# A four-layer graph network whose PSUM banks are dealt out anew: four banks in turn for the work outside the recurrence, one bank shared inside it, and residual sums in pieces

## The chip, the cores and the metric

The kernel runs on one core of a Trainium2 chip. The metric is the device time of one execution in microseconds. The kernel before takes 1431.12 us, the median of three runs (1428.45 to 1432.41).

## What is computed

128 batches of 64 nodes with 256 features pass through four layers. Each layer normalises its input, clips it at zero, computes one graph operation on it and adds the result to its input (the residual sum). Everything is float32.

```python
for layer in (attention_4_heads, attention_1_head, relations, gated_recurrence):
    h = maximum(layernorm(x), 0)
    x = x + layer(h, adj, weights)          # the residual sum

# attention: Wh = h @ W; softmax over the neighbours; elu(attention @ Wh)
# relations: adj is 0 or 1 here, so that only relation 1 is ever met
# gated_recurrence, three steps on the same adjacency A:
    m    = h @ weight[i]
    aggr = A^T @ m
    r = sigmoid(aggr @ Wir + h @ Whr + b)
    z = sigmoid(aggr @ Wiz + h @ Whz + b)
    n = tanh(aggr @ Win + b + r * (h @ Whn + b))
    h = (1 - z) * n + z * h
```

## The kernel before

The rows of all graphs are laid on 128 partitions and taken in 16 groups of four tiles of 128 rows. Per group, the first three layers and the preparation of the recurrence are called "the work outside the recurrence" here. The recurrence of group g runs in three steps, each in two chunks `a` and `b` of 128 output features. Outside work of later groups is placed beside it.

The order in which each engine does its instructions is worked out when the program is built. A planner notes all operations with what they depend on, and then emits, again and again, the one that can start first by its own account of time; among equals the one that is due first. LATENCY, the start and end of each job and its `spread` set those dues. On the chip each engine runs its list in order and waits at semaphores.

PSUM has eight banks of 512 float32 per partition. Five belong to the recurrence, one to each kind of product; three (`mt`) are dealt out in turn to everything else. Until the recurrence is first used, the outside work may also have four of the five.

```python
class Banks(Pool):
    own = ("ry", "rm", "rz", "nh", "ni")
    early = psum = True

    def room(self, tag, base):
        return 3 if tag == "mt" else 1

    def tile(self, shape, dtype, name, **kwargs):
        view = super().tile(shape, dtype, name, **kwargs)
        view.base.whole = name not in self.own     # (*)
        return view

    def place(self, base, taken):
        if base.tag in self.own:
            return super().place(base, taken)
        for tag in ("mt", *self.own[: 4 if 115.0 else 5]) if self.early else ("mt",):
            ...
psum = Banks(..., 1, Banks.own)        # tags in `own` are taken in the order asked for
```

(*) The first TensorE operation on a bank that is marked `whole` waits until the inputs of all TensorE operations on it are there, so that the bank is held shortly. Banks of the recurrence aren't marked: their products are emitted one by one.

In a chunk, `r` (the reset gate) of the first half of the columns, S0, is made from two products in the bank `rm` and two in `ry`, one of each from h and one from the messages. Seven such pairs of products serve both gates of both halves; `ry` is added to over and over and copied out in between, `rz` takes two more. `nh` and `ni` are the two parts of n, from h and from the aggregated messages. Each call of `mul` is one 256-column product, which the chip does as two matmul instructions; each call of `gate` is one of 512 columns, also as two.

```python
class Chunk:
    def __init__(...):
        self.r, self.t, self.z, self.d = (work.tile([P, T], F32, name=name) for name in "rtzd")   # one buffer each

    def bank(self, name):
        if name in self.banks:
            return self.banks[name], False
        self.banks[name] = psum.tile([P, T], F32, name=name)
        return self.banks[name], True

    def nh_there(self):                                 # ScalarE reads nh into t
        nc.scalar.activation(self.t, self.banks["nh"], AF.Identity, bias=bh[...])

    def r_there(self, h):
        r, t = self.r[:, h], self.t[:, h]
        if h == S0:
            nc.vector.tensor_tensor(r, self.banks["rm"][:, S0], r, ALU.add)     # VectorE reads rm
            y = r
        else:
            y = self.banks["ry"][:, S0]
        nc.scalar.activation(r, y, AF.Tanh, bias=brz[...], scale=0.5)
        nc.vector.scalar_tensor_tensor(t, r, 1.0, t, op0=ALU.add, op1=ALU.mult)
    # n_there: t += ni, tanh, d = h - t (GpSimd);  z_there: rz, tanh
    # h_there: d = (z + 1) * d; hnew = d * 0.5 + t

# one step of the recurrence, in the order in which the banks are asked for (cut)
a.mul("ry", 1, 0); a.gate("nh", 0)
...; a.gate("ni", 0); ...; a.gate("nh", 1); a.nh_there()
a.mul("rm", 2, 0) + a.mul("rz", 7, 0); a.mul("rm", 2, 1)
a.r_there(S0); ...; a.both("ry", 6); a.m16_there()
b.both("rm", 2)                                         # b asks for rm first
a.both("ry", 5); ...; b.gate("nh", 0)                   # and for nh after it
a.both("ry", 3); a.r_there(S1); ...; a.h_there(S1); ...; a.h_there(S0)
b.gate("nh", 1); b.nh_there(); b.both("ry", 1); b.m1_there(); b.r_there(S0)
...
```

The two attention layers end with elu and the residual sum, 128x1024 elements for a whole group. From the second group on GpSimd does the sum:

```python
def elu_add(work, src, o, engine, by_scalar=False):
    ...
    nc.vector.scalar_tensor_tensor(em, em, -1.0, o, op0=ALU.add, op1=ALU.max)
    engine.tensor_tensor(src, src, em, ALU.add)
```

Of the kernel before, what the change touches and what calls it, by code (L numbers as in the profile page):

```python
# [8 lines left out]
F32 = mybir.dt.float32  # L9
I32 = mybir.dt.int32  # L10
AF = mybir.ActivationFunctionType
ALU = mybir.AluOpType
# [4 lines left out]
P = 128  # L17
# [3 lines left out]
G = 4  # L21
T = G * P
# [26 lines left out]
class View:  # L49


    def __init__(self, base, shape, steps=(), region=None, live=None):
        self.base, self.shape, self.steps, self.region, self.live = base, tuple(shape), steps, region, live
# [83 lines left out]
class Pool:  # L137
# [3 lines left out]
    psum = False  # L141
# [21 lines left out]
    def released(self, tag, base, before):  # L163
# [3 lines left out]
        if before < 0:  # L167
            return 0.0
        return sorted(b.end for b in live if not b.left)[before] + Plan.LATENCY

# [29 lines left out]
class Job:  # L200
# [2 lines left out]

    def __init__(self, start, end, after):
        self.start, self.end, self.after, self.left, self.length = start, end, after, 0, 0.0
        self.spread = 1.86


class Plan:

    LATENCY = 170.8

    def __init__(self, nc):
        self.nc, self.on, self.ops, self.job = nc, False, [], None
# [51 lines left out]
    def emit(self):  # L268
# [20 lines left out]
        for op in reversed(self.ops):  # L289
            if op.job.end is None:  # L290
                op.due = 1e9
                for t in op.then:
                    late = 0.0 if t.engine == op.engine else self.LATENCY
                    op.due = min(op.due, t.due - op.job.spread * (op.cost + late))
# [8 lines left out]
        def enter(op):  # L303
            t = 0.0
            for other, data in op.after.items():
                late = other.end + self.LATENCY
                if other.engine == op.engine and not (other.dma and data):
# [137 lines left out]
def kernel(  # L445
# [28 lines left out]
    nc = Plan(tc.nc)  # L474
# [141 lines left out]
    def elu_add(work, src, o, engine, by_scalar=False):  # L616

        em = work.tile(list(o.shape), F32, name="em")
        if by_scalar:
            nc.scalar.activation(em, o, AF.Relu, scale=-1.0)  # L620
            nc.scalar.activation(em, em, AF.Exp, scale=-1.0)
        else:
            nc.vector.tensor_scalar(em, o, 0.0, None, op0=ALU.min)
            nc.scalar.activation(em, em, AF.Exp)
        nc.vector.scalar_tensor_tensor(em, em, -1.0, o, op0=ALU.add, op1=ALU.max)
        engine.tensor_tensor(src, src, em, ALU.add)

    def block_diagonal(dst, src, scalar, op):

# [131 lines left out]
    def recurrence(work, psum, start, src, abd, store, in_parts=False):  # L761
# [16 lines left out]
        class Chunk:  # L778
# [8 lines left out]
            def bank(self, name):  # L787

                if name in self.banks:
                    return self.banks[name], False  # L790
                self.banks[name] = psum.tile([P, T], F32, name=name)
                return self.banks[name], True

            def mul(self, name, q, source):
# [157 lines left out]
    with ExitStack() as s1:  # L952
# [4 lines left out]
        class Banks(Pool):  # L957

            own = ("ry", "rm", "rz", "nh", "ni")
            early = psum = True

            def room(self, tag, base):
                return 3 if tag == "mt" else 1

            def tile(self, shape, dtype, name, **kwargs):
                view = super().tile(shape, dtype, name, **kwargs)
# [3 lines left out]
            def place(self, base, taken):  # L972
                if base.tag in self.own:
                    return super().place(base, taken)
                for tag in ("mt", *self.own[: 4 if 115.0 else 5]) if self.early else ("mt",):
                    live = sum(1 for b in self.live.get(tag, ()) if b.left)
                    if live + taken.count(tag) < self.room(tag, base):
                        return tag
                return None
# [7 lines left out]
        psum = Banks(s1.enter_context(tc.tile_pool(name="psum", bufs=1, space=PSUM)), 1, Banks.own)  # L987
# [29 lines left out]
        def load_group(g):  # L1017
            nc.begin(("load", g))
            xg = work.tile([P, G, D], F32, name="xg", bufs=6)
            n = 2 if g == 0 else G  # L1020
            for p in range(0, G, n):
                nc.sync.dma_start(xg[:, p : p + n], xr[:, g * G + p : g * G + p + n, :])
            at = work.tile([P, G // 2, 2, N], I32, name="at", bufs=3)
            for a in range(2):
                for u in range(G // 2):
                    edges = tr[g * G // 2 + u, a]
                    nc.sync.dma_start(at[a * N : (a + 1) * N, u], edges)
            AT.append(at)
            XG.append(xg)
# [71 lines left out]
        def attention(g, p0, n, layer, heads, we, pool):  # L1101
# [49 lines left out]
            for q in range(0, n, m):  # L1151
# [5 lines left out]
                nc.vector.tensor_tensor(t4, t4, edges, ALU.min)  # L1157
            o = aggregate_graphs(pool, psum, t, wv, heads, g < 16)
            elu_add(pool, src, o, nc.vector if g < 1 else nc.gpsimd, g < 0)

        def first_weights():
# [84 lines left out]
        def before(g):  # L1246
            ABD[g] = work.tile([P, G, N], F32, name="abd")
            START[g] = before_recurrence(W[3], psum, XG[g], AG[g], ABD[g], g >= AHEAD)

        def recur(g):  # L1250
            recurrence(
                W[3], psum, START.pop(g), XG[g], ABD[g],
                lambda h, part: nc.sync.dma_start(outr[:, g * G : (g + 1) * G, :][part], h[part]),
                g == NG - 1,
            )
# [3 lines left out]
        nc.begin("weights", 18.0, 0 or None)  # L1259
        later_weights(early)  # L1260
        layers = (first_layer, second_layer, third_layer)
        start, period = 87.96, 83.9
        users = {}
        for g in range(NG):
            if g > 1:
                load_group(g)

            if g == 0:
                units = [(0, 2, (-2.5, 24.3, 61.4, 71.1)), (2, 2, (-2.7, 25.3, 58.8, 74.4))]
            elif g == 1:  # L1270
                units = [(0, 2, (24.1, 54.4, 87.6, 97.3)), (2, 2, (45.5, 67.3, 98.2, 128.1))]
            elif g == 2:
                units = [(0, G, (74.5, 120.77, 176.8, 238.5))]
            else:
                end = start + g * period - 32.8
                units = [(0, G, [end - 53.2 * i + x for i, x in ((3, 0.0), (2, -0.95), (1, -4.68), (0, 0.0))])]
            for p0, n, at in units:
                spare = g == 0 and p0 > 0
                for i in range(3):
                    end = None if g < 2 else at[i + 1]  # L1280
                    nc.begin((g, p0, i), at[i], end, [users[i]] if i in users and not spare else [])
                    if g > 1:
                        nc.job.spread = 3.0
                    if not spare:
                        users[i] = (g, p0, i)
                    layers[i](g, p0, n, spare)
            if g == 0:
                nc.begin("make")
                nc.note("-", make_gru, 0.0, [], [], [op for op in nc.ops if any(b.pool is early for b in op.bases)])
            at = start + g * period  # L1290
            nc.begin(("before", g), at - (13.0 if g == 0 else 21.1), at, [("recur", g - 2)] if g > 1 else [])
            before(g)
            nc.begin(("recur", g), at, at + period)
            recur(g)
# [58 lines left out]
    def general_attention(X):  # L1353

        with ExitStack() as s3:
# [16 lines left out]
            for layer, heads, we in ((0, H, w0e), (1, 1, w1e)):  # L1372
                pool = Plain(str(layer))
                gh = G * heads
                with tc.For_i(0, NP, G) as p0:
# [40 lines left out]
                    for c in range(0, gh, 4):  # L1416
# [3 lines left out]
                        nc.vector.tensor_copy(ec[:, c : c + 4, :].rearrange("p h i -> p (h i)"), pt)  # L1420
                    o = aggregate(pool, psum, lambda p, h: ec[:, p * heads + h, :], wv, heads)
                    elu_add(pool, src, o, nc.gpsimd)
                    nc.sync.dma_start(X[:, bass.ds(p0, G), :], src)

# [115 lines left out]
```

## Time and profile before

| What | Value |
|---|---|
| Time, median of three | 1431.12 us |
| Span of the profiled execution | 1428.7 us |
| TensorE (PE) | busy 1403.0 us, 98% of the span, 9703 matmul instructions |
| VectorE (DVE) | busy 1027.9 us, 72% |
| ScalarE (ACT) | busy 808.1 us, 57% |
| GpSimd (POOL) | busy 600.5 us, 42% |
| TensorE clock granted | 0.997 |
| DMA | 67.89 MB, 48 GB/s |
| First product of the recurrence of the first and second group | 91.7 us, 191.1 us |
| and of the last group | 1349.7 us |

A busy share is the time in which at least one instruction of that engine is under way. The ends of matmuls are modelled and reach over the start of the next one, so that PE at 98% still has short gaps that the share hides: the distance between the starts of two matmuls tells more. In the lists of groups each line gives engine, operation, output<-inputs, shape and count, then busy time and the mean time of one in ns, then the idle time just before them and what ended it.

From some 190 us on the groups follow each other every 82 to 84.5 us; the last group has no outside work left to put beside its recurrence.

### The profile page before, as it was taken

The numbers are of one execution on the slowest core, as the hardware profiler recorded it, in microseconds if no ns is written. First come the engines' busy times: TensorE is split into PE (matmuls) and PEld (weight loads), VectorE is DVE, ScalarE is ACT, GpSimd is POOL, SyncE is SP. The second block draws the span as 40 slices with busy tenths as digits, with TensorE's granted clock in tenths as the row PEclk, the third lists the DMA queues.
The fourth block names the chain that finished last, engine by engine and source line by source line (L and its number), as shares of the span: only waits on it lengthen the run. The fifth ranks groups of instructions, "written<-read, shape, count | busy, mean of one in ns | idle before, by whom it ended". The sixth has DMA issues, their size and how long they took to land.

```text
span 1428.7 us, 27951 instructions
## 1 busy us (share of the span) xinstructions
PE 1403.0 (98%) x9703; PEld 964.6 (68%) x9703; DVE 1027.9 (72%) x2553; ACT 808.1 (57%) x2045; POOL 600.5 (42%) x744
## 2 busy tenths in 40 slices
PE   9999999999999999999999999999999999999997
PEld 8666666767667666766766676676667666666664
DVE  6658677785958869685886968688686958665544
ACT  3665556565555655655565565556556555554543
POOL 1454344445424444543444354344435434352422
PEclk9999999999999999999999999999999999999998
DMA  8010222222223122222312222231212122111000
GB/s 219 22 20 20 42 60 37 59 44 41 61 49 71 32 63 42 45 60 49 72 31 63 42 46 60 48 72 30 59 28 44 45 45 54 26 22 28 16 15 18
DMA packets 299420, 67.89 MB, mean 48 GB/s; under 512 B 274696, under 2 KB 297480, under 8 KB 299272
## 3 DMA queue, kind: packets, MB, share of 16 engines
q1 hardware_dynamic: 298712, 65.50, 22.0%
q8 instruction: 80, 1.31, 0.4%
q14 instruction: 68, 0.56, 0.1%
q10 hardware_dynamic: 560, 0.52, 0.1%
HBM read 28.06 MB, written 8.53 MB: 26 GB/s over the span
## 4 chain that ended last, share of the span: by engine, by line
PE 88%; DVE 5%; ACT 2%; DMA 2%; SPq 1%; issue 1%; POOL 1%; DVEq 0%; ACTq 0%; POOLq 0%
PE ry L388 22%; PE mm L388 16%; PE rz L388 11%; PE ni L388 10%; PE nh L388 10%; PE rm L388 5%; PE tp L388 4%; PE mm L609 3%; PE tp L609 3%; PE ni L1322 2%; DVE t L388 1%; DMA t<-row 1%; SPq L388 1%; DVE d L388 1%; DVE hT L388 1%
## 5 line engine op out<-in xcount | busy, mean ns | idle before, releaser
L388 POOL TENSOR_TENSOR d<-hT,t 128x256 f32<-128x256 f32 x192 | 143.2, 754 | 485.1 <-ACT t L388 479.8
L388 PE MATMUL ni<-aT,wc 128*128 128x512 f32 x384 | 194.6, 595 | 0.0
L388 PE MATMUL nh<-hT,whh 128*128 128x512 f32 x384 | 193.6, 597 | 0.0
L388 DVE SCALAR_TENSOR_TENSOR t<-r,t 128x256 f32<-128x256 f32 x192 | 110.9, 582 | 66.2 <-ACT r L388 43.4
L388 ACT ACTIVATE z<-z,brz 128x256 f32<-128x256 f32 x192 | 96.8, 504 | 90.4 <-DVE z L388 90.2
L388 ACT COPY z<-ry 128x256 f32<-128x256 f32 x192 | 70.9, 369 | 130.3 <-PE ry L388 86.8
L388 POOL TENSOR_TENSOR hS<-hT 128x256 f32<-128x256 f32 x96 | 79.4, 833 | 121.6 <-PE ry L388 84.5
L388 PE MATMUL ry<-hS,wsum 128*128 128x256 f32 x384 | 117.3, 387 | 2.6 <-ACT z L388 2.6
L388 PE MATMUL rz<-hS,whh 128*128 128x256 f32 x384 | 117.5, 388 | 2.2 <-DVE z L388 2.1
L388 ACT ACTIVATE hn<-xg,var,rstd 128x256 f32<-128x256 f32 x200 | 107.4, 594 | 13.1 <-DVE var L388 12.7
L388 PE MATMUL mm<-wl,hT 128*128 128x512 f32 x248 | 114.7, 597 | 0.1
L388 PE MATMUL ry<-aS,wsum 128*128 128x256 f32 x384 | 114.5, 380 | 0.0
L388 PE MATMUL rz<-aS,wc 128*128 128x256 f32 x384 | 114.4, 380 | 0.0
L388 DVE SCALAR_TENSOR_TENSOR hT<-d,t 128x256 f32<-128x256 f32 x192 | 110.8, 593 | 4.3 <-ACT fd L388 0.5
L388 DVE SCALAR_TENSOR_TENSOR d<-z,d 128x256 f32<-128x256 f32 x192 | 101.1, 537 | 17.2 <-ACT z L388 10.5
L388 ACT ACTIVATE t<-t,bi 128x256 f32<-128x256 f32 x192 | 93.9, 502 | 29.2 <-DVE t L388 28.8
L388 DVE TENSOR_TENSOR t<-t,gd 128x512 f32<-128x512 f32 (+2 forms) x48 | 29.8, 645 | 107.8 <-DMA t<-row 95.3
L388 DVE TENSOR_TENSOR z<-rz,z 128x256 f32<-128x256 f32 x192 | 80.0, 417 | 34.3 <-ACT z L388 17.4
L388 PEld LDWEIGHTS ry<-hS,wsum 128*128 128x128 f32 x384 | 69.4, 190 | 44.5 <-issue 25.3
L388 POOL TENSOR_TENSOR aS<-aT,aS 128x256 f32<-128x256 f32 x96 | 74.0, 772 | 57.8 <-ACT aT L388 57.7
L388 DVE BATCH_NORM_STATS2 st<-xg 128x6 f32<-128x256 f32 x256 | 93.3, 408 | 2.7 <-DMA xg<-in_x_dram 2.7
L388 POOL TENSOR_TENSOR hS<-hT,hS 128x256 f32<-128x256 f32 x96 | 74.7, 778 | 43.9 <-DVE hT L388 43.0
(205 smaller groups left out, 3268.9 us busy)
## 6 DMA issues: line engine op xcount, KB each, us to landing
hT<-hn SPq DMA_DIRECT2D x896, 32.0 KB
xg<-in_x_dram SPq DMA_DIRECT2D x15, 512.0 KB
out_dram<-hnat SPq DMA_DIRECT2D x15, 512.0 KB
t<-row SPq DMA_DIRECT2D x28, 256.0 KB
at<-in_adj_dram SPq DMA_DIRECT2D x64, 32.0 KB
eg<-in_adj_dram SPq DMA_DIRECT2D x64, 32.0 KB
ag<-in_adj_dram SPq DMA_DIRECT2D x16, 128.0 KB
t<-row SPq DMA_DIRECT2D x28, 64.0 KB
```

Source lines behind the costliest of these rows:

```text
L388: return do(*[real(a) for a in args], **{k: real(v) for k, v in kwargs.items()})
L609: nc.nc.tensor.matmul(*[real(x) for x in product], start=True, stop=True)
L1322: nc.spare = lambda: psum.early and nc.nc.tensor.matmul(pause, warm, warm, start=True, stop=True)
```

## The change

Eight banks are dealt out anew. The recurrence gives up the bank `rm`: those two products now live in the bank of `nh`, one after the other in the order asked for. The freed bank goes to the outside work, which now has four in turn. As `rm` isn't in `own` any more, its two products count as `whole` and are kept together. The residual sum on GpSimd is cut into one instruction for each tile of 128 rows (128x256 elements), so that a later instruction can go between them. The planner's constants are set anew to fit.

What it is for: more room for the outside work to fill TensorE with, and shorter instructions on GpSimd.

```diff
@@ class Job
-        self.spread = 1.86
+        self.spread = 1.98
@@ class Plan
-    LATENCY = 170.8
+    LATENCY = 172.81
@@ elu_add
-        engine.tensor_tensor(src, src, em, ALU.add)
+        if engine is nc.sync:
+            nc.sync.dma_start(src, em, accum_op=ALU.add)
+        elif engine is nc.gpsimd and 1:
+            for p in range(0, o.shape[1], 1):
+                ps = slice(p, p + 1)
+                engine.tensor_tensor(src[:, ps], src[:, ps], em[:, ps], ALU.add)
+        else:
+            engine.tensor_tensor(src, src, em, ALU.add)
@@ Chunk.bank
-                self.banks[name] = psum.tile([P, T], F32, name=name)
+                self.banks[name] = psum.tile([P, T], F32, name=name, tag="nh" if name == "rm" else name)
@@ Banks
-            own = ("ry", "rm", "rz", "nh", "ni")
+            own = ("ry", "rz", "nh", "ni")
...
-                return 3 if tag == "mt" else 1
+                return 4 if tag == "mt" else 1
...
-                for tag in ("mt", *self.own[: 4 if 115.0 else 5]) if self.early else ("mt",):
+                for tag in ("mt", *self.own[: 3 if 115.0 else 4]) if self.early else ("mt",):
@@ dues of the jobs
-        start, period = 87.96, 83.9
+        start, period = 87.96, 84.63
...
-                units = [(0, G, (74.5, 120.77, 176.8, 238.5))]
+                units = [(0, G, (74.17, 120.77, 182.75, 238.77))]
...
-                units = [(0, G, [end - 53.2 * i + x for i, x in ((3, 0.0), (2, -0.95), (1, -4.68), (0, 0.0))])]
+                units = [(0, G, [end - 52.14 * i + x for i, x in ((3, 0.0), (2, -0.52), (1, -4.27), (0, 0.0))])]
...
-            nc.begin(("before", g), at - (13.0 if g == 0 else 21.1), at, [("recur", g - 2)] if g > 1 else [])
+            nc.begin(("before", g), at - (13.0 if g == 0 else 20.39), at, [("recur", g - 2)] if g > 1 else [])
```

The branch with `nc.sync` is never taken: the sums are called with VectorE for the first group and with GpSimd after it.

## The prediction

> **What bounds the kernel now.** I read the page from the top: busy shares, then the chain that ended last.
>
> ```profile
> PE 1403.0 (98%) x9703; PEld 964.6 (68%) x9703; DVE 1027.9 (72%) x2553; ACT 808.1 (57%) x2045; POOL 600.5 (42%) x744
> PE 88%; DVE 5%; ACT 2%; DMA 2%; SPq 1%; issue 1%; POOL 1%; DVEq 0%; ACTq 0%; POOLq 0%
> ```
>
> PE is busy almost throughout and makes up 88% of the chain. No other engine is above 72%. So time can only be won where PE stands still or is late, and the change takes no product away. The first question is how much standing still is left. The busy times by stage, asked for the ramp, the periods and the last group:
>
> ```profile
> 0.00:88.00 88.00, 86.65 (x635) 66.24 (x636) 56.55 (x192) 48.09 (x141) 28.55 (x46) 1.00 0.37 100
> 88.00:1346.00 1258.00, 1244.79 (x8675) 849.41 (x8674) 933.90 (x2278) 724.67 (x1825) 548.93 (x668) 1.00 0.23 46
> 1346.00:1429.00 83.00, 71.57 (x396) 48.91 (x394) 37.43 (x84) 35.36 (x81) 23.06 (x31) 0.95 0.05 15
> ```
>
> After the stage and its length, the second column is PE. It leaves 13 us idle in the middle 1258 us, but the modelled ends of matmuls overlap the next start and hide gaps. I therefore counted by the step from start to start of equal matmuls: 0.429 us for 512 columns, 0.215 for 256, 0.222 and 0.216 for the 264 and 258 columns of the attention layers, 0.109 for a transpose, about 0.63 us for a block of 32 small products. Times the counts in the list of groups: ry 1536 x 0.215 = 330; rz and rm 1152 x 0.215 = 248; nh, ni and the 512-column ones some 1016 x 0.429 = 436; the attention values 55 + 54; transposes 57; small products 60 + 65; the rest 10. That is 1,315 us of work in 1428.7. Of the other 114 us some 40 lie in the first 88 us, where 32 us of filler products stand for PE with nothing to do, and some 17 in the last group and its final chain. About 55 us remain for the 1258 us between, 4.4%, and much of that is a pause of 60 to 100 ns when a product comes just in time. The waits of PE from 172 to 1263 us, by length, are small too:
>
> ```profile
> PE rm L388 <- DVE r L388: 1.7, 4, 0.7
> PE ry L388 <- ACT z L388: 1.3, 2, 0.8
> PE mm L609 <- DVE t L388: 1.2, 1, 1.2
> ```
>
> So the change plays for a part of the 55 us, and for a little at the two ends.
>
> **What the Trainium skill says.** "PSUM — Partial Sum Buffer", Specifications (TRN2), gives eight banks per partition of 512 FP32 values. The 512-column nh product therefore fills its bank, and rm can't lie beside it, only before or after it; the trace has nh as 128x512, which agrees. The same page, "PSUM bank collisions raise a hardware error", asks that PSUM be guarded by bank: the reader of nh must be done before rm's first product. "SBUF — State Buffer", Who interferes with whom, says of the port pair that VectorE and GpSimd share: a VectorE instruction with two SBUF inputs contends with a GpSimd instruction that reads SBUF, and whoever issues first holds the pair for the whole instruction. The trace of before agrees strikingly. VectorE and GpSimd in order of time, start and length first:
>
> ```profile
> 712.56 0.41 DVE L388 TENSOR_TENSOR z<-rz,z 128x256 f32<-128x256 f32 x1
> 712.89 2.79 DVE L388 SCALAR_TENSOR_TENSOR t<-r,t 128x256 f32<-128x256 f32 x2
> ...
> 712.71 2.35 POOL L388 TENSOR_TENSOR xg<-xg,hn 128x1024 f32<-128x1024 f32 x1 [1.16 <-DVE hn L388]
> ```
>
> The first of two reset-gate steps, begun 0.18 us after the residual sum, can't end before it: the pair takes 2.79 us, where 0.41 each is the usual length. I went through all 32 sums: 27 stretch a t<-r,t, d<-z,d, hT<-d,t or oh<-eg by over 1 us, 53 us in all. [...]From this trace (0.754 us for 256 elements, 2.35 for 1024) a fixed 0.22 us per instruction follows, an estimate: the same order.
>
> **The change, part by part.**
>
> *Sums in pieces.* The rows concerned:
>
> ```profile
> L388 POOL TENSOR_TENSOR xg<-xg,hn 128x1024 f32<-128x1024 f32 (+1 forms) x32 | 71.9, 2247 | 21.2 <-DVE hn L388 21.2
> L388 POOL TENSOR_TENSOR d<-hT,t 128x256 f32<-128x256 f32 x192 | 143.2, 754 | 485.1 <-ACT t L388 479.8
> ```
>
> 14 groups have two sums of four tiles and group 1 has four of two: 28 x 4 + 4 x 2 = 120 pieces. At the 754 ns of the equal-sized d they cost 90.5 us instead of 71.9, so 19 us more on GpSimd, which is idle over half the time. A blocked VectorE instruction now waits for one piece, at most 0.75 us instead of 2.0. What this is worth isn't 53 us: PE stands still for only about 0.26 us beside most of those blocks, as the planner knows of the lock and puts other products there. Only at 182, 211, 1129, 1212 and 1271 us does PE lose 0.6 to 1.5 us nearby. The first normalisation steps of the next layer can also start after one piece. I put 3 us on it: 10 short stalls of 0.26 and a part of the long ones.
>
> *The fourth bank.* The aggregations and attention sums take two banks at once, with three in all only one pair can be under way; a transpose or value product beside it takes the third. Stalls ahead of these products between 130 and 1400 us come to some 20 us by my count of steps, of which half are the pipeline's own. A fourth bank should win a part, and lets the planner put outside work where the recurrence waits: 7 us.
>
> *rm in the bank of nh.* Chunk b of one step, as PE, then VectorE, then ScalarE did it:
>
> ```profile
> 643.24 1.02 PE L388 MATMUL nh<-hT,whh 128*128 128x512 f32 x2
> ...
> 645.82 0.59 PE L388 MATMUL rm<-hT,whh 128*128 128x256 f32 x2
> 646.25 1.02 PE L388 MATMUL nh<-hT,whh 128*128 128x512 f32 x2
> 650.06 0.59 PE L388 MATMUL rm<-aT,wc 128*128 128x256 f32 x2
> ...
> 650.76 0.42 DVE L388 TENSOR_TENSOR r<-rm,r 128x256 f32<-128x256 f32 x1 [0.24 <-PE rm L388]
> ...
> 656.77 0.69 ACT L388 ACTIVATE t<-nh,bh 128x512 f32<-128x512 f32 x1
> ```
>
> nh began 7.5 us before rm was read. In the shared bank it must come after 651.2, where its 1.72 us fit well: ScalarE reads it only at 656.77, because the single buffer t is held until chunk a's h at 656.0. Over the 48 chunks b the room from the reading of rm to that of nh is 5.0 us in the median and below the needed 1.95 us in one. In chunk a the order is nh, then rm. The reading of nh ends 5.6 and 4.8 us (medians) before rm is read in the second and third step, enough for rm's 0.86 us, but 2.2 us after it in the first step. There rm moves back by some 3.4 us (2.2, plus 0.86 of products and two hand-overs of about 0.2), r's first half with it; what follows it, t<-r,t, needed the copy of nh anyway, and moves by 0.86 + 0.42 + 0.51 and hand-overs, some 2.3 us. Half a chunk follows before z is done, so little of it reaches PE. What is lost is freedom: 1.72 us of nh and 0.86 of rm per step are no longer at hand as filler when a's middle waits for its copies. I charge 0.06 us a step, 48 x 0.06 = 3 us; this is a choice, set by the 60 to 100 ns of a just-in-time pause.
>
> *New dues.* They only order what is ready; the wall period of 83.6 us comes from PE's work, so 84.63 isn't a slower clock. I count 1 us for them.
>
> Sum: -3 - 7 + 3 - 1 = -8; 1431 - 8 = 1423 us.
>
> **Rivals.**
> 1. *Nothing to win.* PE is full, GpSimd and banks are off the path; the plan just changes its order. For it: waits of PE below 10 us between 172 and 1263. It gives 1428 to 1434.
> 2. *The shared bank becomes the wait.* Two readers on two engines now pass one bank four times a step. If rm and nh then come just in time, every step loses two pauses and some copies: 0.3 us x 48 = 14 us, 1445. For it: the first step's 2.2 us, and the last group, which has no outside work to fill with. Against it: the 5 us of room.
> 3. *Outside work was starved of banks.* If with three banks work piled up and left PE thin at 1130, 1212, 1271 us and in the two last groups, four banks repair more than the stalls just ahead of their products: a third of the 55 us plus 5 of the ends, some 23 us, 1408.
>
> **Range and chances.** Since products are unchanged, all three lie within 1.6% of the time before. I take 1423, with 1404 to 1440 for eight in ten: rival 3 with a little more at the low end, rival 2 cut to two thirds at the high end. Faster by over 2% needs 29 us, more than half of the middle's gaps: 0.09. Slower by as much needs a shared bank at twice rival 2's price: 0.04.
>
> **What would show it.** Right: PE's work unchanged; the xg sums at x120 and 0.75 us; no reset-gate step over 1.3 us beside them; gaps ahead of small products and transposes halved; periods near 83 us. For rival 2: waits of PE on the reader of nh or rm grow by over 5 us, and the last group lengthens. For rival 3: the outside work ends earlier and the periods fall to 82. I am wrong altogether if periods change by over 1.5 us either way, or if the ramp of 88 us moves by over 5 us.

## The result, and the profile after

The changed kernel takes 1436.15 us, the median of its runs (1434.35 to 1436.27), the kernel before 1430.75 beside it: 1.0036 times as long, 95% interval 1.0019 to 1.0053. It lost 5 us where 8 us of gain were predicted.

The page of the changed kernel, busy shares and the chain that ended last:

```profile
span 1434.5 us, 28074 instructions
PE 1392.9 (97%) x9679; PEld 966.5 (67%) x9679; DVE 1004.6 (70%) x2553; ACT 816.3 (57%) x2045; POOL 623.7 (43%) x832
PE 89%; DVE 3%; ACT 2%; SPq 2%; issue 2%; DMA 1%; POOL 0%; ACTq 0%; DVEq 0%; POOLq 0%
```

PE still makes up most of the chain. It ran 9461 matmuls of the work in both kernels; the 24 that are missing are filler products of the first microseconds (218 in place of 242). VectorE is busy for 23 us less, GpSimd for 23 us more. The rows of the pieces and of the equal-sized d:

```profile
L388 POOL TENSOR_TENSOR xg<-xg,hn 128x256 f32<-128x256 f32 x120 | 94.4, 816 | 42.7 <-DVE hn L388 36.7
L388 POOL TENSOR_TENSOR d<-hT,t 128x256 f32<-128x256 f32 x192 | 146.9, 768 | 445.2 <-ACT t L388 445.2
```

There are 120 pieces of 0.82 us. Between them VectorE gets its turn: its instructions beside the sums take some 25 us longer than usual in all, as against some 56 us before.

Where the 5.8 us between the two profiled spans lie can be read from when each group's first nh product starts. I cut at the first nh product of the fourth group and of the twelfth. Before: 355.3, 669.2 and 404.2 us for the start, the middle and the end. After: 355.9, 668.0 and 410.6. So **the middle is 1.2 us faster and the end 6.4 us slower**. Cut at the first ry<-hS, ni or rz product of these groups instead, the middle differs by 1.1 us at most and the end is 5.9 to 9.8 us slower. Three waits of PE that grew in the end, before and after, in total, times and longest (the longest in total, of transposes for hT, went from 3.9 to 5.4 us):

```profile
PE ry L388 <- ACT z L388: 2.5, 3, 1.2
PE mm L609 <- issue: 0.2, 1, 0.2
```

```profile
PE ry L388 <- ACT z L388: 3.4, 8, 0.5
PE mm L609 <- issue: 3.2, 3, 1.6
PE ry L388 <- POOL aS L388: 3.1, 2, 2.8
```

Two are new or nearly so: attention products (mm), and the sums aS. (hT and aT hold h and the messages, transposed; hS and aS are sums and differences of their parts that GpSimd makes.) Both waits go back to an engine's list that waits for a transfer. GpSimd near the end of group 14, in the changed kernel:

```profile
1334.74 0.73 POOL L388 TENSOR_TENSOR hS<-hT,hS 128x256 f32<-128x256 f32 x1
1338.76 1.41 POOL L388 TENSOR_TENSOR hS<-hT 128x256 f32<-128x256 f32 x2 [3.28 <-issue]
1340.12 0.72 POOL L388 TENSOR_TENSOR aS<-aT,aS 128x256 f32<-128x256 f32 x1
```

The two hS sums at 1338.76 include one for the last group, whose hT arrives by 16 transfers that are issued only from 1324.54 to 1335.3; aS for the running step stands behind it in the list, and PE waits for aS. The view says "issue" here, but the last notice of a landing stands in the trace at 1338.46, 0.3 us before the sum starts. Some 250 us earlier VectorE waits likewise for t, the attention weights, and PE waits for VectorE:

```profile
1088.27 0.72 DVE L388 TENSOR_TENSOR t<-t,gd 128x256 f32<-128x256 f32 x1 [4.54 <-DMA t<-row]
...
1090.82 0.40 PE L609 MATMUL mm<-wh,t 64*64 64x257 f32 x1 [1.36 <-issue]
```

VectorE's last step on t ends at 1090.72, 0.1 us before the product starts. That the planner's own account of time had both transfers there sooner is likely, but not shown.

One count is given for every run that follows. For each kernel I added up the **gaps of PE**: by how much the step from one matmul's start to the next exceeds the usual step of that shape. Before: 77.1 us; after: 82.5. Span less gaps: 1351.6 and 1352.0. As both run the same products, more time is nearly by definition more gaps: the count says how much PE lost, not why. It also hangs on what is taken as the usual step of small products: with each block of them counted as one, the gaps are 66 and 76 us. A few us in it can't be read.

### The profile page after: what moved, and what is told of

It is laid out like the page before. It is cut to its first block, busy times and chain, and to the rows that moved or that the text cites. A ratio compares the mean times of both kernels' runs of the same rounds, so it can differ in the third digit from the quotient of the medians.

```text
span 1434.5 us, 28074 instructions
## 1 busy us (share of the span) xinstructions
PE 1392.9 (97%) x9679; PEld 966.5 (67%) x9679; DVE 1004.6 (70%) x2553; ACT 816.3 (57%) x2045; POOL 623.7 (43%) x832
## 4 chain that ended last, share of the span: by engine, by line
PE 89%; DVE 3%; ACT 2%; SPq 2%; issue 2%; DMA 1%; POOL 0%; ACTq 0%; DVEq 0%; POOLq 0%
PE ry L388 23%; PE mm L388 16%; PE nh L388 11%; PE rz L388 11%; PE ni L388 10%; PE rm L388 5%; PE tp L388 4%; PE mm L609 3%; PE tp L609 3%; SPq L388 2%; PE ni L1329 2%; ACT hn L388 1%; DVE t L388 1%; PE tq L609 1%; PE mn L609 1%
## 5 line engine op out<-in xcount | busy, mean ns | idle before, releaser
L388 POOL TENSOR_TENSOR d<-hT,t 128x256 f32<-128x256 f32 x192 | 146.9, 768 | 445.2 <-ACT t L388 445.2
L388 PE MATMUL nh<-hT,whh 128*128 128x512 f32 x384 | 189.9, 599 | 0.4 <-DVE r L388 0.4
L388 DVE SCALAR_TENSOR_TENSOR t<-r,t 128x256 f32<-128x256 f32 x192 | 106.6, 559 | 68.2 <-ACT r L388 47.8
L388 POOL TENSOR_TENSOR hS<-hT 128x256 f32<-128x256 f32 x96 | 72.5, 762 | 111.5 <-PE ry L388 94.8
L388 DVE TENSOR_TENSOR r<-rm,r 128x256 f32<-128x256 f32 x96 | 40.3, 420 | 110.0 <-PE rm L388 103.2
L388 POOL TENSOR_TENSOR xg<-xg,hn 128x256 f32<-128x256 f32 x120 | 94.4, 816 | 42.7 <-DVE hn L388 36.7
L388 DVE SCALAR_TENSOR_TENSOR d<-z,d 128x256 f32<-128x256 f32 x192 | 96.6, 514 | 19.5 <-ACT z L388 12.3
L388 POOL TENSOR_TENSOR rstd<-var,mhalf 128x4 f32<-128x4 f32 (+1 forms) x70 | 70.4, 1006 | 81.6 <-DVE var L388 68.0
L388 DVE SCALAR_TENSOR_TENSOR hT<-d,t 128x256 f32<-128x256 f32 x192 | 99.8, 530 | 5.8
```

The lines of the kernel that those rows point to most:

```text
L388: return do(*[real(a) for a in args], **{k: real(v) for k, v in kwargs.items()})
```

## The experiments

Theory T: the loss is in the tail. Theory S: the shared bank costs in every step. Theory P: what any part does is mostly what the plan that is made anew with it happens to be. In the table, ratio is to the kernel before, run on the same chip beside it, and differences between runs in the text are mostly taken from these ratios; start, middle and end are as above; all in us. Start, middle, end and gaps are of the one profiled execution, which in e4 was 6 us faster than the median and in e5 3 us slower.

| Run | Time | Ratio, interval | Start | Middle | End | Gaps |
|---|---|---|---|---|---|---|
| before | 1430.75 | | 355.3 | 669.2 | 404.2 | 77 |
| changed | 1436.15 | 1.0036 (1.0019 to 1.0053) | 355.9 | 668.0 | 410.6 | 83 |
| e1 pieces, old order | 1427.88 | 0.9987 (0.9978 to 0.9996) | 354.3 | 667.5 | 403.0 | 73 |
| e2 changed, hold | 1435.80 | 1.0036 (1.0022 to 1.0050) | 355.7 | 672.6 | 406.5 | 80 |
| e3 pieces alone | 1434.23 | 1.0029 (1.0019 to 1.0040) | 365.6 | 665.2 | 402.3 | 80 |
| e4 banks alone | 1464.43 | 1.0247 (1.0225 to 1.0269) | 356.6 | 690.3 | 409.8 | 104 |
| e5 dues alone | 1437.69 | 1.0055 (1.0038 to 1.0072) | 360.2 | 675.7 | 403.1 | 85 |
| e6 sharing alone | 1462.33 | 1.0228 (1.0210 to 1.0246) | 366.7 | 686.7 | 407.5 | 106 |
| e7 changed, old dues | 1448.92 | 1.0134 (1.0117 to 1.0151) | 361.1 | 680.8 | 406.2 | 97 |
| e8 changed, whole sums | 1470.55 | 1.0292 (1.0275 to 1.0309) | 358.1 | 697.1 | 413.4 | 117 |
| e9 nh after rm | 1501.47 | 1.0500 (1.0483 to 1.0518) | 380.4 | 701.0 | 418.1 | 135 |
| e10 rm after nh | 1436.55 | 1.0046 (1.0029 to 1.0062) | 355.7 | 667.0 | 412.1 | 80 |
| e11 order of e8, pieces | 1469.37 | 1.0280 (1.0263 to 1.0297) | 357.4 | 697.5 | 411.7 | 116 |
| e12 changed, three banks | 1489.27 | 1.0421 (1.0404 to 1.0439) | 370.2 | 710.9 | 405.8 | 130 |
| f1 changed again | 1433.83 | 1.0034 (1.0024 to 1.0044) | 355.5 | 668.2 | 408.9 | 81 |
| f2 hold again | 1432.83 | 1.0028 (1.0020 to 1.0037) | 356.7 | 668.8 | 406.8 | 80 |
| f3 hold, rm in turn last | 1434.54 | 1.0034 (1.0022 to 1.0046) | 355.9 | 668.8 | 409.1 | 81 |
| f4 rm in turn | 1447.05 | 1.0123 (1.0108 to 1.0137) | 354.7 | 683.5 | 407.3 | 96 |
| g1 before, LATENCY | 1431.23 | 0.9999 (0.9991 to 1.0008) | 356.6 | 669.3 | 403.6 | 77 |
| g2 changed, LATENCY | 1463.49 | 1.0223 (1.0206 to 1.0240) | 356.0 | 696.8 | 409.6 | 113 |

Span less gaps is 1349 to 1357 us in all rows but e9 (1364.5): the runs differ mainly by what PE loses in gaps.

### Pieces in the old order (e1) and planned anew (e3)

A change of any part makes the planner order thousands of instructions anew. To see the pieces by themselves, e1 lets the planner think of one whole sum and emits four pieces in its place; the order on all other engines stays that of before.

```diff
-        engine.tensor_tensor(src, src, em, ALU.add)
+        def in_pieces():                       # called when the planner emits the one sum
+            for p in range(o.shape[1]):
+                ps = slice(p, p + 1)
+                nc.nc.gpsimd.tensor_tensor(real(src[:, ps]), real(src[:, ps]), real(em[:, ps]), ALU.add)
+        nc.note("Pool", in_pieces, 200.0 + 2.1 * elements(src), [src], [src, em], port=...)
```

> The kernel before, with each residual sum on GpSimd cut into pieces at its own place: the order on every engine stays that of before. This measures the pieces by themselves. Theory A (the pieces free VectorE, worth 3 us as predicted): 1425 to 1429 us. Theory B (PE is full and the planner had put other work beside the lock already): within 1.5 us of 1431. In the trace the t<-r,t beside a sum falls from 2.4 us to 1.3 or less under both.

Measured: 0.9987, some 2 us faster (0.6 to 3.1), which lies in theory A's range. This is the fastest of all the kernels here. VectorE and GpSimd at the place that the prediction showed:

```profile
711.21 0.83 DVE L388 SCALAR_TENSOR_TENSOR t<-r,t 128x256 f32<-128x256 f32 x1
712.31 0.60 DVE L388 SCALAR_TENSOR_TENSOR t<-r,t 128x256 f32<-128x256 f32 x1 [0.27 <-ACT r L388]
...
711.03 3.15 POOL L631 TENSOR_TENSOR xg<-xg,hn 128x256 f32<-128x256 f32 x4 [1.16 <-DVE hn L388]
```

The reset-gate step now waits for one piece, 0.83 us in place of 2.46, and the next is done before the sum ends.

e3 is the change's own form: the planner sees four pieces and orders everything anew (its edit is the change's `for p` loop, nothing else).

> The kernel before with the sums in pieces as the change has them: the planner orders everything anew. Theory A: 1425 to 1429. Theory P (what a part does to the time is mostly what the new plan happens to be): 1425 to 1440, and more than 2 us away from the run with pieces in the old order.

Measured: 1.0029. The same instructions on GpSimd, 6 us apart from e1. The loss lies in the start, 8 to 12 us longer by which product one cuts at. This is what theory P foretold.

### Banks alone (e4) and sharing alone (e6)

```diff
-                self.banks[name] = psum.tile([P, T], F32, name=name)
+                self.banks[name] = psum.tile([P, T], F32, name=name, tag="nh" if name == "rm" else name)
-            own = ("ry", "rm", "rz", "nh", "ni")
+            own = ("ry", "rz", "nh", "ni")
-                for tag in ("mt", *self.own[: 4 if 115.0 else 5]) if self.early else ("mt",):
+                for tag in ("mt", *self.own[: 3 if 115.0 else 4]) if self.early else ("mt",):
 # and in e4 only:
-                return 3 if tag == "mt" else 1
+                return 4 if tag == "mt" else 1
```

> The kernel before with the new dealing of banks alone (rm in the bank of nh, four in turn), with the old constants. Theory S: 1434 to 1440, with the loss spread over the periods. Theory T: the periods from the fourth to the eleventh group stay at 83.5 us, what differs lies in the ramp and in the tail; 1428 to 1440. The prediction's terms (-7 and +3) would give 1427.

> The kernel before with rm in the bank of nh, but still three banks in turn; the eighth bank lies idle. Old dues. Theory S (sharing is what costs in the run of the banks alone, 1464 us): 1460 us or more. Theory F (the fourth bank lets outside work run ahead and crowd the recurrence): 1430 to 1445.

Measured: 34 and 33 us slower. e4 lies far beyond the ranges of both its theories; e6 is as theory S had it. With the old dues and whole sums the sharing costs it all, and the fourth bank gives nothing that can be told from noise (the intervals overlap). The loss is spread over the periods, 85.8 to 86.3 us each in place of 83.6. What PE waits for in e6:

```profile
PE mm L609 <- PE ry L388: 11.2, 12, 1.0
PE ry L388 <- ACT z L388: 9.3, 18, 1.1
PE mm L609 <- issue: 6.6, 7, 1.7
PE ry L388 <- ACT aT L388: 3.6, 3, 2.0
```

### Dues alone (e5), the changed kernel with old dues (e7) and with whole sums (e8), and pieces in the order of e8 (e11)

e5 is the kernel before with the new constants of the change's diff (spread, LATENCY, period and the dues of jobs); e7 is the changed kernel with those constants set back. e8:

```diff
-        elif engine is nc.gpsimd and 1:
+        elif engine is nc.gpsimd and 0:
```

e11 plans as e8 does, with whole sums, and emits pieces in their place, as e1 did.

> The kernel before with the new dues, LATENCY and spread alone: five recurrence banks, three in turn, whole sums. Theory D (the dues belong to the banks and each set fits its own kernel only): slower than before by 5 to 30 us. Theory G (the new dues are better or worse in themselves): about +5 us if they cause the loss, -10 or more if they hide a cost of the banks.

> The changed kernel with the old dues, LATENCY and spread: new banks and pieces. Theory D: 1455 to 1470 as the banks alone. If the pieces repair the banks: 1440 or less.

> The changed kernel with whole residual sums: new banks and dues. Pieces by themselves are worth about 2 us (measured in the old order), so 1438 us if the plan is equally good; theory P (the plan made anew decides): anywhere from 1432 to 1455.

> The changed kernel planned with whole sums (1470.55 us), and in that very order the sums cut into pieces at their place. Theory K (a whole sum locks VectorE while the shared bank waits for it, so that the lock costs more under sharing): 1445 us or less. Theory P (the plan decides; pieces by themselves are worth 2 us): 1467 to 1470.

Measured: 1.0055, 1.0134, 1.0292 and 1.0280. The new dues cost 8 us on the old banks and win 14 on the new ones with pieces (e7 against the change), as theory D has it. e7 lies between its two expectations: the pieces, planned anew, recover some 15 of the banks' 34 us. Taking the pieces out of the changed kernel costs some 36 us, which lies beyond the range of theory P too (1455); putting them back in that plan's own order gives back 1 to 2, not to be told from nothing. So those 36 us are the plan, not the lock on VectorE: theory K falls, and e11 lies in theory P's range. In e8 PE waits longest on the copies of ry:

```profile
PE ry L388 <- ACT z L388: 26.4, 27, 2.2
```

### Each rule of the shared bank without the sharing (e9, e10)

Sharing puts two rules on the order: chunk b's nh after rm of b was read, and chunk a's rm after nh of a was copied. Each can be asked for with all banks as they were. In e9 the code notes nh after the reading of rm and makes it depend on it; in e10 rm depends on the copy of nh, and is kept together.

```diff
 # e9
-            b.gate("nh", 0)                 # between z_there(S1) and the last ry of a
 ...
-            b.gate("nh", 1)
-            b.nh_there()
             b.both("ry", 1)
             b.m1_there()
-            b.r_there(S0)
+            read = b.r_sum()                # r = rm + r
+            for k in range(K):
+                b.gate("nh", k)
+                nc.ops[-1].after.setdefault(read, True)
+            b.nh_there()
+            b.r_rest()                      # tanh, and t
 # e10
+            copied = a.copied               # the operation of a.nh_there()
             a.mul("rm", 2, 0)
+            nc.ops[-1].after.setdefault(copied, True)
 ...
+                view.base.whole = name not in self.own or name == "rm"
```

> The kernel before with its eight banks as they were, and one rule more: chunk b's nh products may start only when its rm bank has been read. No bank is shared; old dues, whole sums. Theory N (sharing costs because nh of chunk b is no longer at hand as filler while PE waits for the copies of ry): 1445 to 1465 us, and the PE waits on ACT z ahead of ry grow from some 5 to over 12 us. Theory H (the hand-over of the bank itself costs): within 5 us of 1430.

> The kernel before with its banks as they were, and the other rule alone: chunk a's rm products start only after nh was copied out, and the products of rm are kept together. Theory N: within 5 us of 1430. If the move of rm in the first step (predicted at 2.3 us on the reset gate) counts: 1440 or more.

Measured: 1.0500 and 1.0046. e9 goes beyond theory N's range, and not in the way that it said: waits on the copies of ry don't grow. PE waits at rm for the state h, and once for 10.5 us on a transfer in the start:

```profile
PE rm L388 <- DVE hT L388: 20.5, 14, 1.8
PE ry L388 <- DMA hT<-hn: 10.5, 1, 10.5
```

The likely reason, which no run shows by itself, is that rm isn't kept together here, unlike in the shared bank, so that rm's first product stands in PE's list ahead of its h. e9 shows that the rule on nh, unfitted, can be expensive; its 71 us can't be taken as what sharing costs. e10 lies between its two expectations. It leaves the middle alone (667.0) and loses 8 us in the end, almost as the changed kernel does.

### The fourth bank (e12) and rm in turn (f4)

```diff
 # e12
-                return 4 if tag == "mt" else 1
+                return 3 if tag == "mt" else 1
 # f4
-                self.banks[name] = psum.tile([P, T], F32, name=name, tag="nh" if name == "rm" else name)
+                self.banks[name] = psum.tile([P, T], F32, name=name)     # rm in any of the four
```

> The changed kernel with three banks in turn in place of four; the eighth lies idle. The predicted worth of the fourth bank (7 us) would give 1443. If the fourth bank is worth nothing, as the two runs with old dues and whole sums say (1464.4 with it, 1462.3 without): 1432 to 1440, plus or minus what another plan does.

> The changed kernel, with rm in any of the four banks in turn in all groups, nh alone in its bank; new dues and pieces. Theory N: nh of chunk b can fill again, so PE gaps fall and the time is 1420 to 1432 if the dues fit. Theory P: the dues were fitted to the shared bank, another plan is worse, 1436 to 1470.

Measured: 1.0421 and 1.0123. Without the fourth bank the changed kernel is 55 us slower, far beyond what was expected; e4 against e6 had it worth nothing. And with nh of chunk b free again (f4), it isn't faster but 13 us slower than the changed kernel beside it. Theory N foretold the opposite, and the time lies in theory P's range. f4 isn't a clean test of N, though: rm now takes one of the outside work's four banks, and its products are still kept together.

### The tail (e2, f1, f2, f3)

e2 and f2 add one dependency to the changed kernel: the last group's hS sums stand behind the running step's aS sums. The order on all other engines is unchanged. (The edit is abridged, with lists of operations in words.) f3 has in addition rm of the last group in one of the four banks in turn. f1 is the changed kernel itself, beside them.

```diff
             before(g)
+            if g == NG - 1:
+                for op in the hS sums of before(g):
+                    op.after.setdefault(the last aS sum of ("recur", g - 1), False)
 # f3 also
-   tag="nh" if name == "rm" else name
+   tag="nh" if name == "rm" and not in_parts else name      # in_parts: the last group
```

> The changed kernel, in which the last group's first hS sums stand behind the running step's aS sums in GpSimd's list; the order on PE, VectorE, ScalarE and of the transfers stays the same. Theory T (the loss lies in the tail: GpSimd's list waits for transfers and holds up ry<-aS for 3.0 us): 1432 to 1434 us, and the PE wait of 2.8 us on aS at 1337 us gone. Theory S (the shared bank costs a little in every step): 1436, only that one wait gone and the time lost elsewhere.

> The changed kernel as it is, side by side with the two next ones: 1436 us, by every theory.

> As e2: the same order, but that GpSimd's list no longer waits for the transfers of the last group before the running step's aS. If gaps of PE in the tail add up to the time: 3 us faster than the changed kernel beside it, 1433. If not, the same time, and something in the body takes it back.

> As f2, and in the last group alone rm lives in one of the four banks in turn, so that nh of chunk b is free to fill PE's waits for the copies of ry again. Theory N at the tail: the 0.63 us gap of PE ahead of ry<-hT,wsum goes in each of the three steps, 1 to 2 us less than f2. If sharing costs nothing in the last group: as f2.

Measured: 1435.80 for e2, the changed kernel's own ratio of 1.0036, as its theory S had it. In the second set, beside each other: 1433.83 for the changed kernel, 1432.83 for f2, 1434.54 for f3; the intervals overlap. The wait on aS is gone in e2 and f2, but it was 3.1 us in one profile of the changed kernel and 0.9 in the other, as the transfers landed sooner there (the last at 1336.22):

```profile
1336.52 1.41 POOL L388 TENSOR_TENSOR hS<-hT 128x256 f32<-128x256 f32 x2 [1.06 <-DMA hT<-hn]
```

So this wait is worth some 1 us of time at most, which can't be told from nothing, and theory T explains little of the loss. f3 plans the last group anew; gaps of 0.63 us ahead of ry<-hT,wsum stay at 1341.00, 1387.91 and 1411.94 us, so nh isn't what used to fill them. e2's profile lost 4 us in the middle at the very same order, which f2's didn't: a difference of 3 us between two profiles can't be read as a cause.

All runs together show more. The last product outside the recurrence (mn<-v,oh) starts at 1316.2 us in the kernel before and at 1313.9 in the changed one, which is ahead up to there. From it to the end the kernel before takes 112.5 us, the changed kernel 120.6, and 118.7 in f1. This stretch takes 111.0 to 113.0 us in the five kernels whose rm has a bank of its own and no further rule (before, e1, e3, e5, g1), and 116.0 to 120.6 in the fifteen others, whatever their dues, pieces and banks in turn, with 616 to 636 matmuls in it. So **the loss of the changed kernel lies where no outside work is left**, and it goes with the new place of rm, not with dues or pieces. In this stretch each of the fifteen has three gaps of some 0.63 us ahead of ry<-hT,wsum; at these places the five have rm products. The last of the three places, before and then changed, PE and ScalarE:

```profile
1407.95 0.59 PE L388 MATMUL ry<-aS,wsum 128*128 128x256 f32 x2
1408.38 0.59 PE L388 MATMUL rm<-hT,whh 128*128 128x256 f32 x2
1408.81 0.59 PE L388 MATMUL rm<-aT,wc 128*128 128x256 f32 x2
1409.24 0.59 PE L388 MATMUL ry<-hT,wsum 128*128 128x256 f32 x2
...
1408.70 0.35 ACT L388 COPY z<-ry 128x256 f32<-128x256 f32 x1
```

```profile
1411.39 0.59 PE L388 MATMUL ry<-aS,wsum 128*128 128x256 f32 x2
1412.45 0.70 PE L388 MATMUL ry<-hT,wsum 128*128 128x256 f32 x2 [0.46 <-ACT z L388]
...
1412.02 0.37 ACT L388 COPY z<-ry 128x256 f32<-128x256 f32 x1
```

Before, rm's products fill PE's time while ScalarE copies ry; in the changed kernel nothing does. e10, f3, f4 and the changed kernel have in common that rm's products are kept together, so that rule is the likely cause; no run changed it alone, and e9, which has the gaps too, has the rule on nh instead. The three gaps make 1.9 us of the 6 to 8. Waits on aS (0.9 and 3.1 us) and longer gaps ahead of transposes of hT (some 1.4 us more) make a part of the rest.

### A constant of no instruction (g1, g2)

```diff
 # g1, on the kernel before
-    LATENCY = 170.8
+    LATENCY = 171.3
 # g2, on the changed kernel
-    LATENCY = 172.81
+    LATENCY = 173.3
```

> The kernel before with LATENCY 171.3 in place of 170.8, a constant of the planner and of no instruction. PE's order differs in a few places, VectorE's and ScalarE's in many. Theory P (the plan decides): 2 to 15 us away from 1430, most likely slower, as the constants were fitted together. If plans of the same structure are equally good: within 1.5 us.

> The changed kernel with LATENCY 173.3 in place of 172.81. Theory P: 3 to 40 us away from 1436, most likely slower, more than in the kernel before, as the shared bank leaves the plan less freedom. If plans of the same structure are equally good: within 1.5 us.

Measured: 0.9999 and 1.0223. In the kernel before PE's list stays nearly the same (12 of 9703 places differ) and so does the time, against theory P; it is hardly another plan, and doesn't say how far plans of that structure lie apart. In the changed kernel 1903 of 9679 places differ, all between 421 and 1112 us, and 27 us are lost with the same banks, pieces and dues. What PE waits for in g2:

```profile
PE mm L609 <- DVE t L388: 11.7, 6, 2.4
PE ry L388 <- ACT z L388: 8.8, 17, 0.9
PE rz L388 <- DVE z L388: 6.7, 12, 0.9
```

g2 is the sharpest evidence for theory P: plans with rm in the bank of nh lie from 1433 to 1489 us, and the change's own, with its variants for the tail, are the lowest of those run. The six plans with a bank for rm, without e9's rule, lie from 1428 to 1438.

## Why the prediction was wrong

**What bounds it** was right. PE ran the same products, the middle kept its period (83.5 us, predicted near 83) and all was decided in the gaps. Rival 1, nothing to win, 1428 to 1434, came nearest; the result lies between it and rival 2. Of rival 2's signs, a longer last group showed in part: 2.6 to 3.1 us longer from its first ry<-hS, ni or rz product to the end, 0.8 us shorter from its first nh product, which the new order places later. The other didn't show: PE waits for the readers of nh and rm 0.4 us in all.

**Sums in pieces**: the mechanism was right and the size nearly so. 120 pieces as counted, 0.82 us each where 0.754 was put; the blocked VectorE step falls to 0.83 us. Worth 2 us in the old order (e1), predicted 3. Ordered anew, the same pieces cost 6 us more than in the old order (e3 against e1).

**The fourth bank, -7 us**: this step failed. Its sign was to be halved gaps ahead of small products and transposes; between 130 and 1400 us they went from some 21 us to some 31, and PE's idle time ahead of the attention products from 1.7 us to 11.7. Added to the sharing with the old dues, the bank gave nothing (e4 against e6); taken out of the changed kernel, it costs 55 us (e12). Neither is its worth apart from a plan. Of rival 3's signs, the outside work did end earlier, by 2.3 us; the periods didn't fall to 82.

**rm in the bank of nh, +3 us**: the step that failed most, by its size. The prediction looked for room in the old order, found 5 us where 1.95 were needed, and so charged "0.06 us a step" for freedom. The room was real: in the changed kernel nh of chunk b starts 1.0 us (median) after rm was read, and is copied 3.8 us after that reading. The loss wasn't a wait on the bank either: ahead of nh PE waits for rm's reader 0.8 us in all at most (g2). The mechanism that the prediction named, rm and nh "no longer at hand as filler", showed for rm, and was charged too little: where no outside work is left, 0.63 us in each of three steps against 0.06; over the whole program the gaps ahead of ry<-hT,wsum grow from 3.4 to 11.2 us, 0.16 us a step. Planned anew with the old dues, the sharing costs 33 us, 0.68 us a step over 48 steps (e6), eleven times the charge. Why the plans of the shared bank are so much worse in the middle stays open: nh as lost filler was tried in three ways (e9, f3, f4), none of them clean, and none bore it out.

**New dues, -1 us**, "they only order what is ready": the other failed step. They cost 8 us on the old banks and are worth 14 on the new ones. The order of what is ready decided these us.

**The end of the program** wasn't in the sum, though rival 2 named the last group. From the last outside product on it takes 6 to 8 us more, which is all of the loss. Shown among its parts are the three gaps where rm used to be (1.9 us) and GpSimd's list waiting for the last group's transfers (1 us of time at most). The attention products that wait before that for t, 4.7 us as against 0.4, cost nothing on balance: from 1024 us to the last outside product PE's gaps are some 14 us in both kernels. The rest stays open.

Eight, then, was a sum of parts that don't add up: -2 for the pieces, +33 for the sharing, and then some -26 that only the refitted plan as a whole brings back. It brought back the middle, but not the end.

## What to carry to other kernels

Where a planner orders the instructions and PE is full, an edit is judged with its plan: change one part at a time in the old order to see what the part does to the hardware, and move a constant of no instruction to see how far plans of the same structure lie apart. A difference that is smaller than this can't be put down to the edit. Look then at the stretch where no other work is left to fill with: here the same three gaps stood there in fifteen different kernels. Cutting GpSimd's two-input sums beside a busy VectorE was worth 2 us here and needed no new order.

## What the runs showed of the hardware

TensorE's clock fell for 3.4 us after gaps of PE that were shorter than that. In e12 from 738 us, by stage: length, PE, and PEclk as the third number from the end of each line:

```profile
738.00:746.40 8.40, 5.30 (x47) 2.87 (x46) 5.22 (x12) 1.19 (x3) 0.00 (x0) 1.00 0.27 45
746.40:749.80 3.40, 3.40 (x39) 2.45 (x38) 2.44 (x9) 1.66 (x4) 1.45 (x2) 0.50 0.00 0
749.80:757.00 7.20, 6.83 (x24) 3.75 (x23) 6.74 (x11) 2.82 (x5) 4.02 (x5) 1.00 0.00 1
```

Steps of 2.26 us between two matmuls, with others of 0.9 us around them, were followed by 3.4 us at a granted clock of 0.5, once in almost every period; products of 256 columns took 0.43 us a step there. "TensorE: Matmul & The Clock Gate" in the Trainium skill (Part 1, What's actually happening) has the clock halved after an idle window of about 3.4 us; here single steps of at most 2.3 us (e12), 2.9 us (g2) and 1.7 us (f1) stood ahead of such stretches. A longer step isn't enough either: 3.43 us in the changed kernel at 1337.5 us, 3.3 in e7 and 3.47 in f4 were followed by none. What decides isn't settled by these runs. Each stretch costs some 1.7 us on top of its gap (an estimate, half of its 3.4 us). In e12 eight of them, one twice as long, make some 15 of its 55 us, in g2 six make some 10 of its 27.
